# A CIN layer on one core: pairs 3 to 15 of its blocks as 32 by 64 matmul tiles, instead of 128 by 128 matmuls with a tiled remainder

## The chip, the cores and the metric

The kernel runs on one core of a Trainium2 chip. The metric is the device time of one execution in microseconds (us); the median of three runs before the change is 733.72 us. The engines are called as the profile calls them: PE (TensorE, matmuls), PEld (its weight loads), DVE (VectorE), ACT (ScalarE), POOL (GpSimd, which issues the gathers) and SP (SyncE, which issues plain DMAs).

## The reference

A batch of 1024 rows, 39 fields (F) and 64 elements (E) goes through three layers, all in float32:

```python
def _cin_layer(Xk, X0, W, b):
    O = W.shape[0]
    Hk, Fdim = (Xk.shape[1], X0.shape[1])
    Wr = W.reshape(O, Hk, Fdim)
    return jnp.einsum('bhe,bfe,ohf->boe', Xk, X0, Wr) + b[None, :, None]
X0 = sparse_embedding
Xk = X0
outs = []
for W, b in ((W0, b0), (W1, b1), (W2, b2)):
    Xk = _cin_layer(Xk, X0, W, b)
    outs.append(Xk.sum(axis=-1))
cin_output = jnp.concatenate(outs, axis=-1)
return cin_output @ fc_w.T + fc_b
```

Only the sums over e reach the output, so the kernel folds layers 2 and 3 and the final product into a second set of weights. What is left to compute for each column (b, e) is, for all unordered pairs of fields (a, b), the product x_a x_b times two sets of 64 weights (W0 and the folded set): 780 pairs and 39 linear terms.

## The kernel before, in words

**Blocks.** The batch is cut into 32 blocks of 32 rows, 2048 columns (32 x 64) each. Two consecutive blocks make a pair: blocks 0 and 1 are pair 1, blocks 30 and 31 are pair 16.

**Data.** `load(n)` copies block n from the input into one of three DRAM tables `xd`, laid out with fields as rows (a pair's two blocks one after the other). POOL then gathers rows of the table into SBUF by index lists (`gather_rows`, line 174): `roll(n)` fills five tiles of 128 partitions by 2048 columns (`rt[n % 2]`, two buffers), each a permutation of the fields with repeats, and `roll_small(n)` fills two tiles of 1024 columns, `ut` and `vt`, for a small remainder.

**Products.** A step (n, c) multiplies two of the five tiles elementwise on DVE (`product`, line 219, out tile `p`, four buffers). Six steps, c = 0 to 5, cover most field pairs in 128 partitions each. The rest of the field pairs fit in 32 partitions; for these the four partition groups of one product hold four column ranges of both blocks of a pair (line 221), so this seventh step comes once in a pair.

**Matmuls.** `multiply` (line 559) does four matmuls of 128 by 128 over 512 columns for a step, one for each of the four PSUM banks of the block (`po`). `join` does the remainder: 16 matmuls of 32 rows by 64 columns of weights (line 579) and, for the linear terms, eight more of the same shape (line 590). Eight such tiles fit side by side in the array. Each float32 matmul stands in the trace as two MATMUL and two LDWEIGHTS records, so a pair has 96 MATMUL records at line 559, 32 at line 579 and 16 at line 590.

**After the sums.** When a block's banks are complete, `finish` turns each of the four with one ACT instruction (line 607) and one DVE instruction (line 609) into a tile `g`, and a DVE reduction (line 620) sums over e, two for a block. ACT copies the fields into `g` (`fields`, line 602).

**Order.** The program is written out by hand, each engine works in order, and semaphores follow from data. The main loop walks the steps of one pair after another: multiply step `at` on PE, then make the product of step `at + AHEAD` (AHEAD is 4) on DVE. The gathers for a later block are emitted behind the last product that reads their buffer. SP's queue holds the loads; `load(n + 4)` waits there until every gather from the table that it overwrites has landed.

Of the kernel before, what the change touches and what calls it, by code (L numbers as in the profile page):

```python
# [39 lines left out]
NY = 3  # L87
YB = B // 4
# [59 lines left out]
def cin_kernel(ctx: ExitStack, tc: tile.TileContext, x, w0t, b0, w1, b1, w2, b2, fc_w, fc_b, out):  # L148
# [28 lines left out]

    def roll(n, tiles=range(NT)):
        for i in tiles:
            k = n % 2 * NT + i  # L180
            gather_rows(rt[n % 2][:, i], xd[n // 2 % NTAB][: FT if k < NT else 2 * FT], k)
# [19 lines left out]
    lists = const.tile([128, 2 * NT + 2], I32, name="lists")  # L201
    rt = [const.tile([128, NT, BLK], F32, name=f"r{k}") for k in range(2)]
# [10 lines left out]
    def product(n, c, cols=slice(0, BLK), p=None):  # L213
        if p is None:
            p = prods.tile([128, BLK], F32, name="p", tag="p")
        if c < NPAIR:
            i, k = PAIRS[c]
            r = rt[n % 2]
# [6 lines left out]
    with prep as prep:  # L225
# [8 lines left out]
        place = prep.tile([128, 1], I32, name="place")  # L234
# [63 lines left out]

        def step(x, at, by, out=None):
# [38 lines left out]
        nc.gpsimd.memset(bothv[0:H, :, F], 0.0)  # L338
        for h in (0, H):
# [40 lines left out]
        r, most, seat, far = (new() for _ in range(4))  # L380
# [92 lines left out]
        nc.vector.tensor_scalar(lists[:, 2 * NT :], both_of, 2.0, seat, ALU.mult, ALU.add)  # L473
        roll_small(0)
# [72 lines left out]
    work = ctx.enter_context(tc.tile_pool(name="work", bufs=2))  # L547
    sums = const.tile([H + F, B], F32, name="sums")
# [48 lines left out]

    def fields(n):
        g[n] = []
        for m in range(BLK // SUB):  # L600
            gt = work.tile([H + F, SUB], F32, name="g", tag="g")
            nc.scalar.copy(gt[H : H + F], rt[n % 2][0:F, 0, bass.ts(m, SUB)])  # L602
            g[n].append(gt)

    def finish_bank(n, m, z):
        one, other = slice(m % 2 * H, m % 2 * H + H), slice((m + 1) % 2 * H, (m + 1) % 2 * H + H)
        nc.scalar.activation(z[one], po[n][m][other], AF.Identity, bias=fc0s[other])  # L607
        at = bass.ts(m % 2, MM)
        return lambda: nc.vector.scalar_tensor_tensor(  # L609
            g[n][m // 2][0:H, at], po[n][m][one], b0s[one], z[one], ALU.add, ALU.mult  # L610
        )

    def finish(n):
        z = [work.tile([128, MM], F32, name="z", tag="z") for _ in range(BLK // SUB)]
        then = [finish_bank(n, m, z[m // 2]) for m in range(BLK // MM)]
        for m in range(BLK // MM):
            then[m]()
            if m % 2:
                b_at = n * BB + m // 2 * SB
                nc.vector.tensor_reduce(  # L620
                    sums[:, b_at : b_at + SB],
                    g[n][m // 2].rearrange("p (b e) -> p b e", e=E),
                    AX.X,
                    ALU.add,
                )

    def finish_quarter(n, m):
        z = work.tile([128, MM], F32, name="z", tag="z")
        finish_bank(n, m, z)()
# [23 lines left out]
    TAIL = 2  # L653
    steps = []
# [151 lines left out]
```

## Time and profile before

| | |
|---|---|
| runs | 732.83, 733.72, 734.34 us; median 733.72 |
| span of the profiled execution | 731.4 us, first to last instruction |
| its own time beside the span | not listed apart from the three runs, which lie 1.4 to 2.9 us above the span |
| PE busy | 724.7 us (99%) |
| DVE busy | 638.3 us (87%) |
| POOL busy | 397.6 us (54%) |
| ACT busy | 166.9 us (23%) |
| moved by DMA | 197.24 MB, mean 270 GB/s |

A row of the groups reads: line, engine, operation, names out<-in, shapes, count, then busy time and the mean of one in ns, then idle time before them. A row of the timeline reads: start, duration, engine, line, operation, count. Matmuls overlap, so the mean duration of one (some 600 ns) is longer than the distance from one start to the next, and it is the distances that add up to the time.

### The profile page before, as it was taken

Reading aid. Unit: us, or ns where it says so; the run is one execution under the profiler, and the core shown is the slowest. Engines: PE = TensorE matmul, PEld = TensorE weight load, DVE = VectorE, ACT = ScalarE, POOL = GpSimd, SP = SyncE. Lnnn points to the kernel's source line nnn. Section 1 sums busy time; section 2 is a strip of 40 time slices with the busy share of each in tenths; the row PEclk is TensorE's granted clock in tenths of the full one; section 3 lists DMA queues with packets and bytes.
Section 4 is the critical chain, followed back from the end, with each engine's and each line's share of the span. In section 5 each row is a group of like instructions: output and inputs, shape, how many; then the busy total and the mean of one; then the engine's idle time right before and its main releaser. Section 6 shows DMA issues by size and latency. Waiting matters only on the chain.

```text
span 731.4 us, 6351 instructions
## 1 busy us (share of the span) xinstructions
PE 724.7 (99%) x2375; PEld 316.1 (43%) x2375; DVE 638.3 (87%) x521; ACT 166.9 (23%) x240; POOL 397.6 (54%) x254
## 2 busy tenths in 40 slices
PE   8999999999999999999999999999999999999998
PEld 4444444444444444444444444444444444444443
DVE  6999798988889988889988889888898988889885
ACT  3332121222212222221222212222121221212222
POOL 6789886536555445754537555455654547545300
PEclk9999999999999999999999999999999999999999
DMA  8997899789575887757679675896767777565700
GB/s 268 376 337 280 315 342 356 290 307 338 232 273 231 281 336 286 270 225 285 269 288 330 223 289 219 304 348 236 268 256 274 301 287 266 224 252 236 288 0 0
DMA packets 65983, 197.24 MB, mean 270 GB/s; under 512 B 40110, under 2 KB 40179, under 8 KB 45984
## 3 DMA queue, kind: packets, MB, share of 16 engines
q0 software_dynamic: 28784, 185.56, 65.5%
q1 hardware_dynamic: 35468, 9.29, 5.5%
q10 hardware_dynamic: 1700, 1.99, 1.0%
q8 instruction: 18, 0.29, 0.1%
q14 instruction: 13, 0.11, 0.0%
HBM read 196.76 MB, written 10.60 MB: 284 GB/s over the span
## 4 chain that ended last, share of the span: by engine, by line
PE 99%; DVE 0%; DMA 0%; issue 0%; ACT 0%; DVEq 0%
PE po L559 91%; PE po L579 4%; PE po L590 2%; PE idle L279 0%; PE pv L406 0%; PE pt L487 0%; PE small L323 0%; PE pv L487 0%; PE pw L418 0%; DMA fcrow<-in_fc_w 0%; PE tr L543 0%; DVE g L609 0%; DVE pairs L526 0%; DVE sums L631 0%; ACT z L607 0%
## 5 line engine op out<-in xcount | busy, mean ns | idle before, releaser
L559 PE MATMUL po<-p,wa 128*128 128x512 f32 x1536 | 666.0, 594 | 0.0
L219 DVE TENSOR_TENSOR p<-r 128x2048 f32<-128x2048 f32 (+2 forms) x198 | 434.1, 2224 | 72.4 <-PE po L559 67.1
L559 PEld LDWEIGHTS po<-p,wa 128*128 128x128 f32 x1536 | 290.5, 190 | 371.7 <-issue 354.6
L174 POOL DMA_INDIRECT r<-xd,lists x156 | 302.3, 1938 | 267.1 <-issue 266.2
L607 ACT ACTIVATE z<-po,columns 64x512 f32<-64x512 f32 x128 | 87.3, 682 | 380.1 <-PE po L590 217.9
L609 DVE SCALAR_TENSOR_TENSOR g<-po,b0s,z 64x512 f32<-64x512 f32 x128 | 95.9, 749 | 9.3 <-ACT z L607 5.3
L602 ACT COPY g<-r 39x1024 f32<-39x1024 f32 x64 | 66.7, 1043 | 155.0 <-DVE sums L620 126.8
L620 DVE TENSOR_REDUCE sums<-g 103x16 f32<-103x1024 f32 x62 | 75.6, 1220 | 2.1
L174 POOL DMA_INDIRECT u<-xd,lists x16 | 38.9, 2432 | 7.5 <-issue 4.6
L174 POOL DMA_INDIRECT v<-xd,lists x16 | 38.5, 2403 | 4.9 <-issue 4.9
L579 PE MATMUL po<-p,wa 32*64 32x512 f32 x512 | 31.6, 600 | 0.0
L221 DVE TENSOR_TENSOR p<-u,v 128x1024 f32<-128x1024 f32 x16 | 19.5, 1218 | 0.0
L579 PEld LDWEIGHTS po<-p,wa 32*64 32x64 f32 x512 | 9.4, 131 | 20.2 <-issue 19.4
L590 PE MATMUL po<-u,wa 32*64 32x512 f32 x256 | 17.0, 587 | 0.0
L174 POOL DMA_INDIRECT r<-xh,lists x8 | 8.0, 996 | 4.8 <-DVE tmp L387 2.7
L590 PEld LDWEIGHTS po<-u,wa 32*64 32x64 f32 x256 | 5.7, 132 | 8.0 <-issue 8.0
L526 DVE TENSOR_TENSOR pairs<-both 128x2 f32<-128x2 f32 (+27 forms) x59 | 6.1, 171 | 0.2
L544 ACT COPY wa<-tr 128x128 f32<-128x128 f32 x8 | 2.1, 266 | 16.2 <-PE tr L543 16.2
L279 PE MATMUL idle<-const-float32-1.0 128*128 128x256 f32 (+1 forms) x8 | 4.0, 596 | 0.8 <-PEq L793 0.8
L543 PE MATMUL tr<-unit,pairs 128*128 128x128 f32 x8 | 2.4, 294 | 2.2 <-DVE pairs L526 2.2
L543 PEld LDWEIGHTS tr<-unit,pairs 128*128 128x128 f32 x8 | 1.2, 151 | 4.7 <-ACT pairs L524 2.7
L168 POOL DMA_DIRECT2D xd<-in_x x3 | 3.2, 1055 | 0.0
(97 smaller groups left out, 56.7 us busy)
## 6 DMA issues: line engine op xcount, KB each, us to landing
xd<-in_x SPq DMA_DIRECT2D x28, 312.0 KB
r<-xd,lists POOLq DMA_INDIRECT x156, 8.9
xd<-in_x POOLq DMA_DIRECT2D x3, 312.0 KB, 7.6
w2s<-in_w ACTq DMA_DIRECT2D x1, 624.0 KB
w1s<-in_w ACTq DMA_DIRECT2D x1, 624.0 KB
w0s<-in_w0t ACTq DMA_DIRECT2D x1, 380.2 KB
xh<-in_x ACTq DMA_DIRECT2D x2, 156.0 KB
xd<-xh SPq DMA_DIRECT2D x2, 156.0 KB
```

What stands on the lines that cost most here:

```text
L174: nc.gpsimd.indirect_dma_start(dst, None, table, bass.IndirectOffsetOnAxis(ap=lists[:, k : k + 1], axis=0))
L219: nc.vector.tensor_tensor(p[:, cols], r[:, i, cols], r[:, k, cols], ALU.mult)
L221: nc.vector.tensor_tensor(p[:, 0:SUB], ut[n // 2 % 2], vt[n // 2 % 2], ALU.mult)
L279: nc.tensor.matmul(idle[:, 0:cols], nc.const_aps.tensor(1.0, (128, 128), F32), nc.const_aps.tensor(1.0, (128, cols), F32), start=True, sto ...
L526: nc.vector.tensor_tensor(out, diagonal(a, b, sa, sb), diagonal(b, a, sb, sa), ALU.add)
L559: nc.tensor.matmul(po[n][m], wa[:, c, side : side + 2 * H], p[:, bass.ts(m, MM)], start=n % 2 == 0 and c == 0, stop=n % 2 == 1 and c == NP ...
L579: nc.tensor.matmul(dst[half * H : half * H + H], wa[rows, NPAIR, at : at + H], p[rows, bass.ts(side, MM)], start=t >= 2, stop=t < 2 and ha ...
L590: nc.tensor.matmul(dst[half : half + H], wa[rows, NPAIR + 1, H : 2 * H], ut[n // 2 % 2][rows, bass.ts(side, MM)], start=False, stop=t < 2,)
L602: nc.scalar.copy(gt[H : H + F], rt[n % 2][0:F, 0, bass.ts(m, SUB)])
L607: nc.scalar.activation(z[one], po[n][m][other], AF.Identity, bias=fc0s[other])
L609: return lambda: nc.vector.scalar_tensor_tensor(g[n][m // 2][0:H, at], po[n][m][one], b0s[one], z[one], ALU.add, ALU.mult)
L620: nc.vector.tensor_reduce(sums[:, b_at : b_at + SB], g[n][m // 2].rearrange("p (b e) -> p b e", e=E), AX.X, ALU.add,)
```

## The change

Pairs 1, 2 and 16 stay as they are. In pairs 3 to 15 (13 pairs) every matmul has the 32 by 64 form. A pair's 4096 columns are cut into four ranges of 1024, one for each group of 32 partitions. A gathered slot is a tile of 128 partitions by 1024 columns, in which group s holds 32 fields of range s; 14 such slots (`slot`, `gather_slots`) take the place of the 12 gathered tiles. Four slots with shifts 0 to 3 times one slot with shift 3, 7, 11, 15 or 19 give a product of 4 x 512 columns with one DVE instruction whose second operand is broadcast (`part_product`); a sixth group is made of the slots with the seven left fields, and one half-size step ("odd") is the rest. A pair has 13 steps as before: 12 products of 2048 columns and one of 1024.

Each unit of 512 columns of such a product is multiplied by eight matmuls, four partition groups by two halves (`part_multiply`), and the linear terms by eight more (`part_linear`). Four groups go to four banks; a pair has two sets of four, one for each half of the columns.

The weights are put in order once, during pair 2: `part_rows` copies and adds them into `pairs` with 21 DVE and 6 ACT instructions, `part_turns` transposes them with 7 PE transposes into `wc`, and 12 DMAs on SP copy them to the other three partition groups (`wn`). The index list of the slots, `narrow`, is worked out in the prologue by 14 POOL memsets and 16 small DVE instructions. Field rows of `g` come by four DMAs for a pair from the table (`part_fields`) instead of four ACT copies, and the reductions are spread over later steps, one to a step.

The order of PE in the middle of a pair before, from the end of the remainder's tiles (L579, L590) to the next full matmuls:

```order
L579 MATMUL po<-p,wa 64x512
L579 MATMUL po<-p,wa 64x512 [waits Activation_49]
L579 MATMUL po<-p,wa 64x512
L590 MATMUL po<-u_87,wa 64x512 [waits DMASW7_49]
L590 MATMUL po<-u_87,wa 64x512 x7
L559 MATMUL po<-p,wa 128x512 [waits DVE_49]
L559 MATMUL po<-p,wa 128x512 x3
L559 MATMUL po<-p,wa 128x512 [waits DVE_49]
```

The order of PE in the changed kernel in the middle of pair 3: the linear terms (L767), and behind them the next product's matmuls (L754), with weights from `wc` or `wn`:

```order
L767 MATMUL po<-r_87,wn 64x512 [waits DMASW2_49]
L767 MATMUL po<-r_87,wn 64x512
L767 MATMUL po<-r_87,wc 64x512 x2
L767 MATMUL po<-r_87,wn 64x512 x4
L754 MATMUL po<-p,wc 64x512 [waits DVE_49]
L754 MATMUL po<-p,wc 64x512
L754 MATMUL po<-p,wn 64x512 x8
L754 MATMUL po<-p,wc 64x512 x2
```

The form no longer alternates with a 128-row one, and an instruction covers a quarter of the rows and half of the weight columns.

PE at the border of pairs 2 and 3 before (the first two rows are the last step but one of pair 2, and the wait for ACT is that for free banks):

```order
L559 MATMUL po<-p,wa 128x512 [waits DVE_49]
L559 MATMUL po<-p,wa 128x512 x3
L559 MATMUL po<-p,wa 128x512 [waits DVE_49]
L559 MATMUL po<-p,wa 128x512 x3
L559 MATMUL po<-p,wa 128x512 [waits DVE_49,Activation_49]
L559 MATMUL po<-p,wa 128x512 [waits Activation_49] x3
```

PE at the same border in the changed kernel, from the last transposes (L679) on; L569 is the former L559, and a DMAHW wait is one for a DMA that SP issued:

```order
L679 MATMUL po<-unit,pairs 128x128 x2
L569 MATMUL po<-p,wa 128x512 x8
L569 MATMUL po<-p,wa 128x512 [waits DVE_49]
L569 MATMUL po<-p,wa 128x512 x3
L569 MATMUL po<-p,wa 128x512 [waits DVE_49]
L569 MATMUL po<-p,wa 128x512 x3
L754 MATMUL po<-p,wc 64x512 [waits DVE_49,Activation_49,Pool_49]
L754 MATMUL po<-p,wc 64x512
L754 MATMUL po<-p,wn 64x512 [waits DMAHW7_49,Activation_49]
L754 MATMUL po<-p,wn 64x512
L754 MATMUL po<-p,wn 64x512 [waits DMAHW0_49,PE_49]
```

Transposes stand four steps ahead of the border, and the first matmuls behind it wait for the copies of the weights.

SP's queue before, from the first load of pair 3's successor on (`xd_68`, `xd_69`, `xd_70` are the three tables; a DMASW wait is one for a gather):

```order
L168 DMA xd_68<-in_x 1248x1x64 [waits DMASW6_49,DMASW5_49,DMASW7_49,DMASW4_49,DMAHW3_49,DMASW3_49,DMAHW6_49,DMASW2_49,DMAHW7_49,DMASW1_49,DMASW0_49]
L168 DMA xd_68<-in_x 1248x1x64 [waits DMAHW4_49]
L168 DMA xd_69<-in_x 1248x1x64 [waits DMASW4_49,DMASW5_49,DMASW3_49,DMASW6_49,DMASW2_49,DMAHW1_49,DMASW1_49,DMASW0_49]
L168 DMA xd_69<-in_x 1248x1x64 [waits DMAHW2_49]
L168 DMA xd_70<-in_x 1248x1x64 [waits DMASW4_49,DMASW5_49,DMASW3_49,DMASW6_49,DMASW2_49,DMASW7_49,DMASW1_49,DMASW0_49]
```

SP's queue in the changed kernel at the same place (L134 is the former L168):

```order
L134 DMA xd_68<-in_x 1248x1x64 [waits DMASW6_49,DMASW5_49,DMASW7_49,DMASW4_49,DMAHW3_49,DMASW3_49,DMAHW6_49,DMASW2_49,DMAHW7_49,DMASW1_49,DMASW0_49]
L134 DMA xd_69<-in_x 1248x1x64 [waits DMASW5_49,DMASW4_49,DMASW6_49,DMASW3_49,DMAHW1_49,DMASW2_49,DMAHW4_49,DMASW1_49,DMASW0_49]
L134 DMA xd_69<-in_x 1248x1x64 [waits DMAHW2_49]
L134 DMA xd_68<-in_x 1248x1x64
L689 DMA wn<-wc 32x896 [waits DVE_49,Activation_49,Pool_49]
L689 DMA wn<-wc 32x896 [waits DMAHW0_49]
L689 DMA wn<-wc 32x896 x2
L689 DMA wn<-wc 32x896 [waits DMAHW3_49]
L689 DMA wn<-wc 32x896 [waits DMAHW4_49]
L689 DMA wn<-wc 32x896 [waits DMAHW5_49]
L689 DMA wn<-wc 32x896 [waits DMAHW6_49]
```

The second load into `xd_68` (block 7) moved behind the two into `xd_69` (blocks 8 and 9), and the twelve copies of the weights stand behind all of them. SP and ACT hand out eight DMAHW numbers in turn, so that a DMA waits for the eighth before it. The first copy has number 7 (PE waits for it above), so the load of block 7 has number 6, and the eighth copy waits until that load has landed.

The diff's core (the shapes of the slots and the weights' 27 runs in `part_rows` are left out):

```diff
+TILES = 4
+ROWS = 128 // TILES
+NPART = NBLK // 2
+WHOLE = (0, 1, NPART - 1)
+SHIFT = (0, 1, 2, 3, 7, 11, 15, 19)
+NK, NG5 = 4, 5
...
+    def part_turns(k):
+        open_part(k, 0)
+        for q in range(NTURN):
+            at = q % 4 * 128
+            nc.tensor.transpose(po[2 * k][q // 4][:, at : at + 128], pairs[:, q], unit)
...
+        for u in range(TILES):
+            for s in range(TILES):
+                if s != u:
+                    nc.sync.dma_start(
+                        wn[ROWS * s : ROWS * s + ROWS, u], wc[ROWS * u : ROWS * u + ROWS]
+                    )
...
+    def gather_slots(k, *which):
+        table = xd[k % NTAB].rearrange("f (t c) -> (f t) c", c=SUB)
+        for j in which:
+            nc.gpsimd.indirect_dma_start(
+                slot(k, j),
+                None,
+                table,
+                bass.IndirectOffsetOnAxis(ap=narrow[:, j : j + 1], axis=0),
+            )
+
+    def part_product(k, group, side):
+        p = prods.tile([128, BLK], F32, name="p", tag="p")
...
+        nc.vector.tensor_tensor(
+            p.rearrange("p (k c) -> p k c", k=NK),
+            slots(k, many, NK, side),
+            slot(k, one)[:, bass.ts(side, MM)].unsqueeze(1).to_broadcast([128, NK, MM]),
+            ALU.mult,
+        )
+        return p, [(NK * group + j, side) for j in range(NK)]
...
+    def weights(c, s):
+        q, u = c // TILES, c % TILES
+        rows = slice(ROWS * s, ROWS * s + ROWS)
+        return wc[rows, q] if s == u else wn[rows, u, q]
+
+    def part_multiply(k, units, p, last):
+        for u, (c, side) in enumerate(units):
+            open_part(k, side)
...
+            for s in range(TILES):
+                rows = slice(ROWS * s, ROWS * s + ROWS)
+                for half in range(2):
+                    kind = (s + side + half) % 2 * H
+                    nc.tensor.matmul(
+                        po[2 * k + side][s][half * H : half * H + H],
+                        weights(c, s)[:, kind : kind + H],
+                        p[rows, bass.ts(u, MM)],
...
+    PART = (
+        *((0, 0), (1, 0), (0, 1), (1, 1), (2, 0), (2, 1), (3, 0), (3, 1), ("odd", 0)),
+        *((4, 0), (5, 0), (4, 1), (5, 1)),
+    )
     steps = []
-    for n in range(0, NBLK, 2):
-        steps += [(n, c) for c in range(NPAIR + 1)] + [(n + 1, c) for c in range(NPAIR)]
+    for k in range(NPART):
+        steps += whole_steps(k) if k in WHOLE else [(k, *t) for t in PART]
...
+        if (n, c) == (2, 0):
+            rows_due.extend(part_rows())
+        if (n, c) == (3, 1):
+            part_turns(first_part)
+
+    def part_step(k, group, side):
...
+        part_multiply(k, units_of.pop(step), p.pop(step), tail)
+        if (group, side) == (0, 1):
+            part_linear(k)
...
+        if tail:
+            part_finish(k, side)
+            sums_due.extend((k, side, b) for b in range(2))
...
+        middle = (2, 1) if len(step) == 3 else (NPAIR,)
+        k = step[0] if len(step) == 3 else step[0] // 2
+        if step[1:] == middle and 1 <= k and k + 3 < NPART:
+            load(2 * k + 6)
+            load(2 * k + 7)
```

More of the change, by code (lines that the diff above doesn't have):

```diff
@@ L338, in cin_kernel @@
         nc.gpsimd.memset(bothv[0:H, :, F], 0.0)
+        slot_shifts()
         for h in (0, H):
@@ L379, in cin_kernel @@
             )
-        r, most, seat, far = (new() for _ in range(4))
+        r, most, far = (new() for _ in range(3))
         both_of = prep.tile([128, 2], F32, name="both_of")
```

315 lines of the change are left out of this document (282 added, 33 removed).

## The prediction

> **What bounds the kernel now.** I read the page's busy line and chain first: is there one engine whose work is the time?
>
> ```profile
> PE 724.7 (99%) x2375; PEld 316.1 (43%) x2375; DVE 638.3 (87%) x521; ACT 166.9 (23%) x240; POOL 397.6 (54%) x254
> PE 99%; DVE 0%; DMA 0%; issue 0%; ACT 0%; DVEq 0%
> PE po L559 91%; PE po L579 4%; PE po L590 2%; PE idle L279 0%; PE pv L406 0%; PE pt L487 0%; PE small L323 0%; PE pv L487 0%; PE pw L418 0%; DMA fcrow<-in_fc_w 0%; PE tr L543 0%; DVE g L609 0%; DVE pairs L526 0%; DVE sums L631 0%; ACT z L607 0%
> ```
>
> PE is the chain from end to end: whatever makes PE quicker is gained in full, whatever makes it wait is paid in full. So the next view is PE's timeline, around one remainder and between two full matmuls far apart (starts first, durations second; the last row is the next pair's remainder).
>
> ```profile
> 348.81 0.59 PE L559 MATMUL po<-p,wa 128*128 128x512 f32 x1
> 349.34 1.97 PE L579 MATMUL po<-p,wa 32*64 32x512 f32 x32
> 351.53 0.63 PE L590 MATMUL po<-u,wa 32*64 32x512 f32 x8
> 352.10 4.13 PE L559 MATMUL po<-p,wa 128*128 128x512 f32 x9
> ...
> 359.50 1.02 PE L559 MATMUL po<-p,wa 128*128 128x512 f32 x2
> 384.82 0.59 PE L559 MATMUL po<-p,wa 128*128 128x512 f32 x1
> ...
> 393.49 1.97 PE L579 MATMUL po<-p,wa 32*64 32x512 f32 x32
> ```
>
> 384.82 - 359.50 = 25.32 us is 59 starts of 0.429 us. I call one such record, or a group of eight small ones side by side, a pass. The weight loads show that the small groups have the same beat:
>
> ```profile
> 349.82 0.18 PEld L579 LDWEIGHTS po<-p,wa 32*64 32x64 f32 x8 [0.25 <-issue]
> 350.25 0.18 PEld L579 LDWEIGHTS po<-p,wa 32*64 32x64 f32 x8 [0.25 <-issue]
> ```
>
> 0.43 us for eight. A pair has 96 + 48/8 = 102 passes: 43.76 us. From remainder to remainder it takes 393.49 - 349.34 = 44.15. The other 0.39 us is the change of form: 0.53 from the last full start to the first small one (0.10 too much), 0.57 from the last small group to the next full one (0.14 too much), the rest on the passes just behind.
>
> **The change: matmuls.** A changed pair has 50 units and one set for the linear terms, each eight tiles, each tile two records: 102 passes again. So the array's work is the same, and what goes is the change of form. Before there are 16 remainders; after, three (pairs 1, 2, 16) and one entry and one exit for all of pairs 3 to 15, so 4. 12 x 0.39 = 4.7 us gained, all of it on PE.
>
> Issue: a pass takes 16 PE instructions instead of two, 26.8 ns for each. The 96 instructions of one remainder take 352.10 - 349.34 = 2.76 us, 28.75 ns each, but that is the array's beat, and a queue could have held some. A burst behind a wait is nearer to the bare rate:
>
> ```profile
> 4.84 0.29 PEld L406 LDWEIGHTS pv<-w2s,fc 128*64 128x64 f32 x3 [0.27 <-DVE wide L362]
> 4.87 0.80 PE L406 MATMUL pv<-w2s,fc 128*64 128x320 f32 x2
> ```
>
> Both rows are of a window that ends at 4.90: five instructions have started within 0.06 us of 4.84, 12 to 15 ns each. I take the issue as hidden, at 0; the two ends are 0 and 16 x 28.75 = 0.46 us a pass, 0.031 x 13 x 102 = 41 us. [...]
>
> **Weights.** Seven transposes are added in pair 2. One in the prologue:
>
> ```profile
> 36.48 1.02 PE L559 MATMUL po<-p,wa 128*128 128x512 f32 x2
> 37.34 0.27 PE L543 MATMUL tr<-unit,pairs 128*128 128x128 f32 x1
> 37.45 1.02 PE L559 MATMUL po<-p,wa 128*128 128x512 f32 x2
> ```
>
> 0.11 us from its start to the next: 7 x 0.11 = 0.8 us, on PE. Their 21 DVE adds and 6 ACT copies are spread over pair 2 and bounded by DVE's spare time in a pair, below; I cost them at 0.
>
> **The entry of pair 3.** PE's first small tiles of pair 3 need the twelve copies `wn`, and these are last in SP's queue. PE in pair 2 (the first row is behind its remainder, the second its last record, with pair 3's first 0.43 us later), SP, POOL, and the page's row of POOL's loads (at its end the us from issue to landing):
>
> ```profile
> 87.15 7.13 PE L559 MATMUL po<-p,wa 128*128 128x512 f32 x16
> 107.42 1.02 PE L559 MATMUL po<-p,wa 128*128 128x512 f32 x2
> ...
> 89.11 0.78 SPq L168 DMA_DIRECT2D xd<-in_x  x1
> 89.94 9.61 SPq L168 DMA_DIRECT2D xd<-in_x  x1
> ...
> 82.00 1.04 POOL L168 DMA_DIRECT2D xd<-in_x  x1
> 92.39 0.94 POOL L174 DMA_INDIRECT r<-xd,lists  x1 [0.31 <-issue]
> 94.87 10.41 POOL L174 DMA_INDIRECT v<-xd,lists  x1 [0.30 <-issue]
> xd<-in_x POOLq DMA_DIRECT2D x3, 312.0 KB, 7.6
> ```
>
> Pair 3 begins at 107.85 before, 108.65 with the transposes. SP issues the loads of blocks 8 and 9 at 89.11 and 89.94 (they wait for pair 2's gathers, which the change leaves), and the second blocks SP for 9.61 us. New behind them: the load of block 7, and only then the twelve copies. How fast do loads come through beside gathers? The queues' shares (packets, MB, share of 16 engines; q0 is POOL's, q1 is SP's), in the windows 92 to 102, 93 to 106, 125.5 to 143.5 and 162.5 to 166.5 us:
>
> ```profile
> q0 software_dynamic: 547, 4.01, 94.8%
> q1 hardware_dynamic: 680, 0.17, 7.6%
> ...
> q0 software_dynamic: 643, 4.09, 74.8%
> q1 hardware_dynamic: 2522, 0.64, 21.7%
> ...
> q0 software_dynamic: 907, 5.46, 73.8%
> q1 hardware_dynamic: 2522, 0.64, 15.7%
> ...
> q1 hardware_dynamic: 2522, 0.64, 70.3%
> ```
>
> Two loads are 2522 packets. Alone they need 70.3% of 4 us, 2.8 us; beside gathers 13 to 18 us. Three are 3783 packets: 4.2 us alone, 20 to 27 us by the two contended windows, so from 93 to 113 or 120. The engines share out packets, not bytes (680 of SP's to 547 of POOL's), and POOL's take nearly all the time. [...]
>
> What limits this: pair 3's gathers are 14 x 128 x 4 KB = 7.3 MB, at 0.40 MB/us 18 us. All wait for block 5's load now, since a slot takes rows of both blocks: 82.00 + 7.6 = 89.6, so they run from some 91.5 to 110. Pair 4's gathers wait for block 7's load, so the pause that frees SP's packets comes then: 91.5 + 18.3 + 4.2 = 114 for the end of the load. I take 113, between the two ways. The eighth copy is issued only once that load has landed (its DMAHW number). What a small DMA of SP needs:
>
> ```profile
> 728.38 0.76 SPq L753 DMA_DIRECT2D out_y<-y  x1
> ```
>
> The output is issued at 728.38, and the span ends at 731.4: at most 3.0 us. 113 + 1 + 3 = 117 for the eighth copy, which PE wants at 108.65 + 4 x 0.43 = 110.4. The wait is 6.5 us, most of it at the first copy already. Its ends: 0, if the copies land by 108.65 (POOL slow, so that loads slip through), and 12, if the load ends at 119.
>
> Behind a wait PE's clock is lower. After 2.18 us of idling in the prologue (second row: PE's busy us behind the length, and near the end the granted clock):
>
> ```profile
> 16.43 0.30 PE L543 MATMUL tr<-unit,pairs 128*128 128x128 f32 x1 [2.18 <-DVE pairs L526]
> 16.50:20.00 3.50, 3.50 (x7) 1.54 (x8) 3.50 (x19) 0.96 (x6) 2.89 (x3) 0.55 1.02 389
> ```
>
> 3.5 us at 0.55 lose 1.6 us. I add 1.5 here, with 0 and 1.6 as ends. While PE waits, DVE can make only the four products it has buffers for, and POOL goes on; nothing is late next.
>
> **Steady pairs.** One pair (PE, PEld, DVE, ACT, POOL busy, clock, DMA share, GB/s), the small gathers, which have the new shape, the instruction queue, and two DVE groups of the prologue:
>
> ```profile
> 172.70:216.86 44.16, 44.16 (x145) 19.11 (x145) 38.94 (x25) 9.63 (x12) 23.39 (x12) 1.00 0.75 276
> L174 POOL DMA_INDIRECT u<-xd,lists x16 | 38.9, 2432 | 7.5 <-issue 4.6 <-DVE p L219 2.9
> q8 instruction: 18, 0.29, 0.1%
> L496 DVE STREAM_TRANSPOSE flat<-pt 128x320 f32<-128x320 f32 x2 | 1.0, 518 | 2.1 <-PE pt L487 2.1
> L526 DVE TENSOR_TENSOR pairs<-both 128x2 f32<-128x2 f32 (+27 forms) x59 | 6.1, 171 | 0.2
> ```
>
> DVE has 25 instructions for a pair as before, 38.94 us, beside a pair now 43.76 long: 4.8 us spare, and four products ahead. POOL issues 14 gathers instead of 12, at most 14 x 2.43 = 34 us. Gathered bytes fall from 11.5 to 7.3 MB, four field copies of 160 KB come back. ACT loses four copies. All hidden: 0; were DVE to run into PE, its cover is those 4.8 us. Instructions arrive in 16 KB pieces (0.29 MB in 18); PE's go from 288 to 1632 for a pair, and even six times the pieces are 1.7 MB beside 190, with a quarter of the DMA time free: 0. The prologue's list is 16 small DVE operations, 16 x 0.17 = 2.7 us by the last row, where DVE waits 2.1 us for PE by the row above it: 0 to 0.6, I take 0, since PE itself is waited for there; its memsets are POOL's, ahead of gathers that wait for the input.
>
> **Sum.** Span 731.4 - 4.7 + 0.8 + 6.5 + 1.5 = 735.5, 4.1 us more. The median of the runs, 733.72, lies 2.3 above the span; with the same 4.1, 737.8 us.
>
> **Rivals.**
> - The copies come in time: the wait is under 2.3 us. Mechanism: POOL's gathers in the new shape are slow (2.43 + 0.30 us, 14 in 38 us, 0.19 MB/us), so DMA is half free and 3783 packets take some 9 us, 93 to 102; copies land at 107. For it: that mean. Against: the row at 92.39 with 0.94 us, and that gathers before fill the engines to 94.8%. Then 733.7 - 4.7 + 0.8 + (0 to 2.3) = 729.8 to 732.2; likeliest 730. The turning point: load 7 ended by about 107.
> - A wait of 2.3 to 3.6 us cancels the gain with the clock's loss: 732.3 to 735.1, no change.
> - PE is bound by issue. For it: eight times the instructions. Against: the burst. 733.7 - 3.9 + 41 = 771 us, whatever the entry does.
> - Little changes because the change of form costs as much inside the small form (weights from two tiles, four banks): then only the entry is left, and it is slower still; within the forecast's upper part.
>
> **Chances.** A wait of 3.6 to 12 us: 0.55, forecast 737.8, its own range 735 to 743.5. The copies in time: 0.25. In between: 0.11. Issue: 0.07. Anything else that leaves the time: 0.02. What a measurement tells from no change is 0.2%, 1.5 us. Faster 0.25, same 0.13, slower 0.55 + 0.07 = 0.62. The range takes the first three cases: 730.0 to 743.5.
>
> **What would show it.** In the trace after: starts of small groups at 0.43 us throughout (step one) and no 0.53 or 0.57 in pairs 3 to 15; 43.8 us a pair. Before pair 3 an idle PE with a DMA of `wn` as the releaser, 6 us long, then some 3.5 us at half clock. POOL's gathers of pair 4 start after block 7's load, near 114. The prediction is wrong if PE idles less than 2 us there, if groups stand 0.46 us apart or more, or if PE waits for DVE or gathers in later pairs.

## The result: 761.26 us, and the profile after

The changed kernel takes 761.26 us (median of 6 runs, 758.0 to 765.34), the kernel before beside it 733.95 (6 runs, 732.83 to 736.21): a ratio of 1.037, interval 1.034 to 1.040. The prediction was 737.8, with 743.5 as its upper end. Ratios below leave out runs over 1.5% above the fastest of their kernel, and medians do not, so that the two can differ.

The page of the changed kernel, its busy line and its chain by engine:

```profile
PE 732.3 (96%) x11118; PEld 336.8 (44%) x11118; DVE 633.5 (83%) x558; ACT 114.5 (15%) x196; POOL 508.8 (67%) x294
issue 30%; POOL 30%; PE 16%; DMA 10%; DVE 2%; SPq 1%; ACT 0%; POOLq 0%; DVEq 0%; ACTq 0%
```

Before, the chain was 99% PE. Now POOL has 30% of it, and PE 16%. The waits of PE and of DVE (us in total, times, longest) say what PE lacks:

```profile
PE po L754 <- DVE p L722: 15.6, 10, 2.3
PE po L754 <- DMA wn<-wc: 2.6, 2, 1.4
PE po L754 <- DVE p L726: 1.8, 8, 0.2
...
DVE p L722 <- DMA v<-xd,narrow: 79.7, 10, 8.4
```

Ten times, once in each of pairs 5 to 14, PE waits for the odd product (L722), and this product has waited some 8 us for the slot `v`, which POOL gathers. The wait that was predicted, for the copies `wn`, is there too.

**The pairs.** The linear terms (L767) come once in a pair, so the distance of their first records is a pair's length. Windows from one to the next, the pairs that start at 169.63, 213.40 and 353.31 (us, then busy PE, PEld, DVE, ACT, POOL, granted clock, DMA share, GB/s):

```profile
169.63:213.40 43.77, 43.77 (x828) 29.22 (x820) 37.90 (x26) 5.46 (x8) 31.07 (x14) 1.00 0.57 188
213.40:259.33 45.93, 45.10 (x833) 22.91 (x824) 37.62 (x26) 5.46 (x8) 31.74 (x15) 1.00 0.59 190
353.31:398.75 45.44, 44.29 (x825) 18.39 (x817) 37.33 (x26) 5.47 (x8) 31.44 (x15) 1.00 0.60 192
```

The first of these is as predicted, 43.77, and so is the pair ahead of it, 43.78. The next ten, pairs 5 to 14, take 464.0 us (213.40 to 677.41) instead of 437.8. That is 26.2 us, nearly the whole loss. The third row shows that neither DVE (37.33 busy) nor POOL (31.44) is full.

**What holds `v`.** POOL, DVE and PE in the third of these pairs (start, duration, count, idle time before):

```profile
348.30 14.72 POOL L712 DMA_INDIRECT r<-xd,narrow  x1 [0.30 <-issue]
363.32 0.94 POOL L712 DMA_INDIRECT r<-xd,narrow  x1 [0.30 <-issue]
364.56 0.94 POOL L712 DMA_INDIRECT v<-xd,narrow  x1 [0.30 <-issue]
```

```profile
347.74 4.47 DVE L726 TENSOR_TENSOR p<-r 128x2048 f32<-128x2048 f32 x2
352.14 1.20 DVE L800 TENSOR_REDUCE sums<-pairs 103x16 f32<-103x1024 f32 x1
353.27 2.27 DVE L726 TENSOR_TENSOR p<-r 128x2048 f32<-128x2048 f32 x1
...
359.93 2.27 DVE L726 TENSOR_TENSOR p<-r,u 128x2048 f32<-128x2048 f32 x1
362.12 1.20 DVE L800 TENSOR_REDUCE sums<-g 103x16 f32<-103x1024 f32 x1
371.18 1.23 DVE L722 TENSOR_TENSOR p<-u,v 128x1024 f32<-128x1024 f32 x1 [7.86 <-DMA v<-xd,narrow]
```

```profile
372.46 0.64 PE L754 MATMUL po<-p,wc 32*64 32x512 f32 x2 [0.92 <-DVE p L722]
```

A gather that nothing holds takes POOL 0.94 us. One in each pair takes 14.72. It lies under a run of DVE in which product, product, then four reductions and three products by turns follow each other without a pause, and it ends at 363.02, 0.82 us behind the end of the last product (359.93 + 2.27 = 362.20). The gather of `v` is the second behind it. The transfers thin out meanwhile and then come all at once (same columns as above):

```profile
353.31:366.00 12.69, 12.69 (x248) 5.48 (x240) 10.02 (x7) 0.00 (x0) 11.78 (x4) 1.00 0.29 90
366.00:372.50 6.50, 5.58 (x109) 2.05 (x94) 1.32 (x2) 0.00 (x0) 2.63 (x3) 1.00 0.99 331
```

The DMA share is 0.29, then 0.99; `v` lands at 371.2, the product follows, and PE has idled by then. The group of these gathers shows none of it:

```profile
L712 POOL DMA_INDIRECT r<-xd,narrow x130 | 319.7, 2459 | 155.2 <-DVE p L726 111.9
```

The mean is 2459 ns, and the prediction's from the kernel before was 2432.

In the kernel before, the longest gather of a steady pair is this one, beside these products:

```profile
362.51 4.47 POOL L174 DMA_INDIRECT r<-xd,lists  x1 [7.77 <-issue]
363.89 4.53 DVE L219 TENSOR_TENSOR p<-r 128x2048 f32<-128x2048 f32 x2
```

It also ends 0.8 us behind a product (363.89 + 2.29 = 366.18; gather's end 366.98). There a reduction followed its finishing instructions; the change took the reductions from there and put one into each of the later steps, between products. That is in the diff (`sums_due`), and the prediction gave it no term.

**The entry of pair 3.** SP's rows, then the queues' shares of the DMA engines (packets, MB, share) in 92 to 100 and in 100 to 115 us:

```profile
91.04 3.23 SPq L134 DMA_DIRECT2D xd<-in_x  x3
100.21 7.79 SPq L689 DMA_DIRECT2D wn<-wc  x12
```

```profile
q1 hardware_dynamic: 3783, 0.96, 52.8%
q0 software_dynamic: 311, 1.16, 42.3%
...
q0 software_dynamic: 735, 2.68, 63.5%
q1 hardware_dynamic: 592, 1.41, 36.9%
```

All 3783 packets of the three loads are through by 100, not by 113. The twelve copies are issued one behind the other, 0.65 us each, from 100.21 to 108.0, and share the engines with pair 3's gathers. What the first of them waits for is on ACT, which copies the transposed weights from PSUM to `wc`:

```profile
98.10 1.04 ACT L811 COPY g<-r 39x1024 f32<-39x1024 f32 x1 [1.78 <-DVE sums L834]
99.17 0.97 ACT L682 COPY wc<-po 128x512 f32<-128x512 f32 x2
```

The transposes are done at 94.55, but ahead of the copy to `wc` ACT has a field copy that waits for a DVE reduction; `wc` is ready at 100.14, and SP issues 0.07 us later. PE from pair 2's remainder on, and windows from pair 3's start on:

```profile
83.69 1.97 PE L589 MATMUL po<-p,wa 32*64 32x512 f32 x32
93.43 1.12 PE L679 MATMUL po<-unit,pairs 128*128 128x128 f32 x7
108.21 0.64 PE L754 MATMUL po<-p,wc 32*64 32x512 f32 x2
111.39 1.18 PE L754 MATMUL po<-p,wn 32*64 32x512 f32 x6 [1.21 <-DMA wn<-wc]
115.19 2.36 PE L754 MATMUL po<-p,wn 32*64 32x512 f32 x6 [1.39 <-DMA wn<-wc]
125.85 0.59 PE L767 MATMUL po<-r,wn 32*64 32x512 f32 x2
108.20:121.54 13.34, 10.75 (x105) 4.70 (x112) 12.83 (x9) 0.69 (x2) 11.51 (x7) 0.74 1.03 272
115.19:121.54 6.35, 6.35 (x52) 3.33 (x60) 6.11 (x5) 0.00 (x0) 5.72 (x3) 0.51 1.03 300
```

From the start to the linear terms are 24 passes, 10.30 us. They took 17.64: the entry loses 7.34 us. Of these 2.6 are idle time that the waits show; 6.35 us at a granted clock of 0.51 lose some 3.1, an estimate; the other 1.6 lie ahead of 115.19, where the matmuls start in pieces behind the copies. The 7.34 us are called the entry's loss below. It doesn't count what is lost ahead of the first product of pair 3; for that, the way from pair 2's remainder (L589) to the linear terms is given too, here 125.85 - 83.69 = 42.2 us.

### The profile page after: what moved, and what is told of

Its sections match the earlier page's. It is cut to its first block, busy times and chain, and to the rows that moved or that the text cites. A ratio compares the mean times of both kernels' runs of the same rounds, so it can differ in the third digit from the quotient of the medians.

```text
span 761.0 us, 24003 instructions
## 1 busy us (share of the span) xinstructions
PE 732.3 (96%) x11118; PEld 336.8 (44%) x11118; DVE 633.5 (83%) x558; ACT 114.5 (15%) x196; POOL 508.8 (67%) x294
## 3 DMA queue, kind: packets, MB, share of 16 engines
q8 instruction: 87, 1.43, 0.8%
## 4 chain that ended last, share of the span: by engine, by line
issue 30%; POOL 30%; PE 16%; DMA 10%; DVE 2%; SPq 1%; ACT 0%; POOLq 0%; DVEq 0%; ACTq 0%
POOL r L712 26%; PE po L754 10%; DMA r<-xd,narrow 7%; PE po L569 5%; POOL u L712 2%; POOL v L712 2%; DMA wn<-wc 1%; DMA r<-xd,lists 1%; SPq L689 1%; DMA v<-xd,narrow 1%; DVE g L818 0%; DVE sums L834 0%; DVE p L191 0%; DVE p L726 0%; PE po L589 0%
## 5 line engine op out<-in xcount | busy, mean ns | idle before, releaser
L754 PE MATMUL po<-p,wn 32*64 32x512 f32 x7800 | 575.5, 593 | 2.6 <-DMA wn<-wc 2.6
L754 PE MATMUL po<-p,wc 32*64 32x512 f32 x2600 | 556.6, 593 | 17.4 <-DVE p L722 15.6
L712 POOL DMA_INDIRECT r<-xd,narrow x130 | 319.7, 2459 | 155.2 <-DVE p L726 111.9
L754 PEld LDWEIGHTS po<-p,wn 32*64 32x64 f32 x7800 | 247.3, 133 | 219.1 <-issue 186.0
L754 PEld LDWEIGHTS po<-p,wc 32*64 32x64 f32 x2600 | 171.6, 133 | 108.1 <-issue 64.5
L726 DVE TENSOR_TENSOR p<-r 128x2048 f32<-128x2048 f32 x78 | 176.0, 2282 | 6.5 <-PE po L754 2.4
L569 PE MATMUL po<-p,wa 128*128 128x512 f32 x288 | 126.8, 597 | 0.0
L726 DVE TENSOR_TENSOR p<-r,u 128x2048 f32<-128x2048 f32 x52 | 118.5, 2280 | 3.9 <-PE po L754 3.9
L722 DVE TENSOR_TENSOR p<-u,v 128x1024 f32<-128x1024 f32 x13 | 15.9, 1224 | 86.4 <-DMA v<-xd,narrow 79.7
L191 DVE TENSOR_TENSOR p<-r 128x2048 f32<-128x2048 f32 (+2 forms) x42 | 81.7, 1978 | 6.7 <-DMA r<-xd,lists 5.7
L569 PEld LDWEIGHTS po<-p,wa 128*128 128x128 f32 x288 | 54.1, 191 | 68.5 <-issue 63.8
L140 POOL DMA_INDIRECT r<-xd,lists x26 | 65.4, 2517 | 12.3 <-issue 6.7
L726 DVE TENSOR_TENSOR p<-r,v 128x2048 f32<-128x2048 f32 x26 | 59.4, 2284 | 4.5 <-PE po L754 4.5
L140 POOL DMA_INDIRECT u<-xd,lists x3 | 17.0, 5683 | 2.3 <-DVE p L191 1.7
```

The lines of the kernel that those rows point to most:

```text
L140: nc.gpsimd.indirect_dma_start(dst, None, table, bass.IndirectOffsetOnAxis(ap=lists[:, k : k + 1], axis=0))
L191: nc.vector.tensor_tensor(p[:, cols], r[:, i, cols], r[:, k, cols], ALU.mult)
L569: nc.tensor.matmul(po[n][m], wa[:, c, side : side + 2 * H], p[:, bass.ts(m, MM)], start=n % 2 == 0 and c == 0, stop=n % 2 == 1 and c == NP ...
L712: nc.gpsimd.indirect_dma_start(slot(k, j), None, table, bass.IndirectOffsetOnAxis(ap=narrow[:, j : j + 1], axis=0),)
L722: nc.vector.tensor_tensor(p[:, 0:SUB], slot(k, LEFT), slot(k, RIGHT + NK), ALU.mult)
L726: nc.vector.tensor_tensor(p.rearrange("p (k c) -> p k c", k=NK), slots(k, many, NK, side), slot(k, one)[:, bass.ts(side, MM)].unsqueeze(1) ...
```

## The experiments

The theory: the lone reductions between products keep POOL's gather out, and what stands behind it comes late. The rivals: the new slots or products by themselves; DVE is simply too busy; the order of the gathers; the entry, whose delay is carried on. All runs are timed beside the kernel before; diffs are against the changed kernel.

**Reductions back beside the finishing instructions (e1).** `part_sum` right behind each two instructions of `part_finish`:

```diff
+            if s % 2:
+                part_sum(k, side, s // 2)
...
-            sums_due.extend((k, side, b) for b in range(2))
```

> The changed kernel, with the four reductions of a pair back beside the finishing instructions, two behind each pair of them, instead of one to a step between products. Theory (DVE's run without a gap, two products and then product and reduction by turns, keeps one POOL gather waiting 14.7 us in every pair, and the two slots of the odd product are behind it): the run is broken by the finishing instructions and by waits for PE, no gather takes over 8 us, the odd product stops waiting for v, pairs take 43.8 us, and the 26 us of pairs 5 to 15 go: 735 to 738 us. Rival (fourteen gathers a pair are simply too many for POOL, at 2.3 us each beside DVE): 758 to 762 us, as it is. Second rival (reductions in a burst make products late, and PE waits for DVE instead): 740 to 758 us, with PE waiting for products other than the odd one.

Measured: 750.18 us, ratio 1.022 (1.015 to 1.028). No wait for the odd product is left. But a long hold is, elsewhere (POOL and DVE):

```profile
347.57 12.61 POOL L712 DMA_INDIRECT v<-xd,narrow  x1 [0.31 <-issue]
348.29 6.69 DVE L726 TENSOR_TENSOR p<-r 128x2048 f32<-128x2048 f32 x3
354.89 4.49 DVE L726 TENSOR_TENSOR p<-r,u 128x2048 f32<-128x2048 f32 x2
```

Five products in a row hold as well (359.38 + 0.8 = 360.18). So lone reductions are not needed for a hold: here a run of products does it. Each pair takes 44.63 us, 0.86 too much. In the pair shown it is lost between 345.5 and 347.7, where PE begins the next pair's third product and DVE's finishing instructions, now with reductions between them, end at 347.11; that PE waits there for the banks that they free is argued from these times and not shown. The expected 735 to 738 us did not come. The time lies in the range of the second rival, but its sign is missing: PE has no wait for a product in pairs 3 to 15.

**The odd product's slots ahead of the right ones (e2).** In the list of the last step's gathers:

```diff
-                (5, 1): (LEFT, *range(RIGHT, RIGHT + NK + 1)),
+                (5, 1): (LEFT, RIGHT + NK, *range(RIGHT, RIGHT + NK)),
```

> The changed kernel, with one gather moved: the second slot of the odd product is gathered ahead of the four slots of the sixth group instead of behind them. Nothing else moves, and the count is the same. Theory: the gather held 14 to 15 us is still there in every pair, but the odd product's slots are ahead of it, so DVE doesn't wait 8 us for v, and what is behind the hold is wanted later: 735 to 740 us. Rival (too many gathers): the same POOL time is only met at another product, 756 to 762 us.

Measured: 735.63 to 758.95 in nine runs, median 751.25; the ratio of 1.0066 (1.0037 to 1.0095) is that of the three shortest, up to 742.16. In the profiled execution, a long one of 748.06, nine pairs take 43.77 or 43.78 though the hold is there,

```profile
344.16 14.73 POOL L712 DMA_INDIRECT r<-xd,narrow  x1 [0.30 <-issue]
```

since what it delays is now used later. e12 below, with the same order, shows it in a whole execution: a hold of 14.72 us in each pair, and all pairs at 43.77 or 43.78. So it is not the hold that costs, but what is behind it in POOL's queue. The version has no margin: later in the execution of 748.06 us the hold grows to 19.2 us, and pairs to 47.9.

**Copies ahead of the loads (e3).** Loads 7, 8 and 9 are issued behind the twelve copies:

```diff
-        if c == 0 and n in (2, 3):
+        if c == 0 and n == 2:
...
+            for m in (7, 8, 9):
+                load(m)
...
-        if step[1:] == middle and 1 <= k and k + 3 < NPART:
+        if step[1:] == middle and 2 <= k and k + 3 < NPART:
```

> The changed kernel, with the loads of blocks 7, 8 and 9 put behind the twelve copies of the weights in SP's queue instead of ahead of them. Theory of the entry (PE loses 7.3 us there, waiting for copies that stand behind three loads, and by the lower clock after it): the loss falls to under 1.5 us. If the rest is as it was: 754 to 756 us. Rival: from pair 5 on POOL's gathers set the pace, so that an earlier entry is only waited for later: 758 to 761 us, although the entry's loss is gone.

Measured: 762.74 us, 1.038 (1.034 to 1.042). Neither of the two expected ranges came. The copies are issued at 103.70, in e2 at 103.62 (both executions reach pair 2's remainder 2.5 to 3 us later than the changed kernel's); ACT's copy to `wc` ends at 103.63: it was not the loads that they waited for. The entry's loss falls to 1.72, but PE waits 3.08 us for the first product of pair 3, and from pair 2's remainder to the linear terms are 40.2 us, only 2.0 fewer than in the changed kernel. The steady pairs lose no less than there (20.3 us of waits for the odd product, 15.6 there). The entry is a matter of its own.

**The kernel before, its reductions spread one to a step (e5).**

```diff
-            if m % 2:
-                ... nc.vector.tensor_reduce(...)
+        sums_due.extend((n, m) for m in range(2))
...
+        if sums_due and at - 1 not in over:
+            due = sums_due.pop(0)
+            sum_up(*due)
```

> The kernel before, with its reductions taken from beside the finishing instructions and put one to a step behind products, as the change does. Theory (a run of DVE without a gap holds a gather): gathers longer than 8 us appear in every pair, where the longest in steady pairs was 4.5; the kernel before has 20 us of POOL's time to spare in a pair, so the time is 732 to 738 us. Rival (the long gather belongs to the new slots, their count or their rows): no gather in steady pairs over 5 us, 732 to 736 us.

Measured: 736.6 us, 1.0048 (1.0033 to 1.0063). The longest gather from 110 us on is 5.22 us, and 2.28 from 130 on, not over 8: a miss. In the kernel before it is 4.48 there, so the holds became shorter. DVE and POOL, in a stretch of 11.4 us without a pause (356.44 to 367.81: product, product, then reduction and product twice by turns):

```profile
360.85 1.21 DVE L624 TENSOR_REDUCE sums<-g 103x16 f32<-103x1024 f32 x1
362.04 2.34 DVE L219 TENSOR_TENSOR p<-r 128x2048 f32<-128x2048 f32 x1
362.05 0.94 POOL L174 DMA_INDIRECT r<-xd,lists  x1 [0.30 <-issue]
```

Five gathers pass in this stretch, none above 2.27 us. So lone reductions and a DVE without pauses do not make a hold of 14 us by themselves. The rival's sign (no gather over 5 us in steady pairs) is met, but its cause, the new slots, is not: in the changed kernel a gather of the old form (L140, at 673.22) is held for 19.18 us beside the new products. A rival that no run tries is the form of the product itself, whose second operand is now broadcast (L726).

**Shorter reductions (e7).** Each reduces 16 of 64 elements:

```diff
-            g[k, side, b].rearrange("p (h b e) -> p h b e", h=2, e=E),
+            g[k, side, b].rearrange("p (h b e) -> p h b e", h=2, e=E)[:, :, :, 0 : E // 4],
```

> The changed kernel, with the four reductions of pairs 3 to 15 cut to the first 16 of 64 elements of each row (three quarters of the reduction are left out); gathers, products and order are the same. DVE has 3.6 us less to do in a pair. Theory (what holds POOL is DVE's run without a gap): the run ends sooner, the held gather takes under 12 us instead of 14.7, the waits for the odd product fall by more than half: 735 to 748 us. Rival (the number of gathers alone): 757 to 762 us.

Measured: 739.11 us, 1.0079 (1.0049 to 1.0109); every pair takes 43.77 or 43.78. The hold is 9.81 us and ends when DVE, quicker now, runs out of work and waits 1.03 us for PE. Less work on DVE cures it, then; this alone would also fit a DVE that is too busy.

**Reductions by twos (e13).** The same reductions, the same DVE work, two behind each other instead of one:

```diff
-            due = sums_due.pop(0)
+            for _ in range(2 if len(sums_due[0]) == 3 else 1):
+                due = sums_due.pop(0)
```

> The changed kernel with the reductions two to a step, so that two stand together between products, instead of one and one. It tells what keeps POOL out between two products. If POOL gets in whenever DVE has no product under way, a 2.4 us stretch of reductions lets the held gather go after the first or second pair of products: under 8 us instead of 14.7, and the time falls to 735 to 755 us. If POOL is kept out for as long as a next product already stands ready behind the running instructions, the hold stays at 14 to 17 us and the time at 755 to 764 us.

Measured: 737.67 us, 1.0036 (1.0008 to 1.0065). POOL, DVE and one steady pair:

```profile
340.69 4.74 POOL L712 DMA_INDIRECT r<-xd,narrow  x1 [0.31 <-issue]
345.74 4.15 POOL L712 DMA_INDIRECT v<-xd,narrow  x1 [0.30 <-issue]
350.19 7.49 POOL L712 DMA_INDIRECT r<-xd,narrow  x1 [0.30 <-DVE sums L800]
```

```profile
340.14 4.48 DVE L726 TENSOR_TENSOR p<-r 128x2048 f32<-128x2048 f32 x2
344.54 1.21 DVE L800 TENSOR_REDUCE sums<-pairs 103x16 f32<-103x1024 f32 x1
345.67 1.20 DVE L800 TENSOR_REDUCE sums<-both 103x16 f32<-103x1024 f32 x1
346.79 2.27 DVE L726 TENSOR_TENSOR p<-r 128x2048 f32<-128x2048 f32 x1
```

```profile
608.31:652.08 43.77, 43.77 (x830) 19.58 (x822) 38.50 (x26) 5.46 (x8) 24.95 (x12) 1.00 0.54 175
```

The first gather ends at 345.43, 0.81 behind the two products; no wait for the odd product is left; all pairs take 43.77 or 43.78, with DVE as busy as ever (38.50). This separates the theory from "DVE too busy": only the places of the reductions differ, and DVE has no more pauses in this stretch than before. The numbers are now those of the prediction: span 736.5 (735.5 predicted), entry's loss 8.0 (8.0 predicted, of other parts).

**Slots by SP instead of POOL (e6).** Four of the 14 slots come by 16 plain DMAs:

```diff
+                nc.sync.dma_start(
+                    slot(k, j)[ROWS * s : ROWS * s + ROWS],
+                    xd[k % NTAB][first : first + ROWS, s % 2 * SUB : s % 2 * SUB + SUB],
+                )
```

> The changed kernel, with four of a pair's fourteen slots (shifts 0 to 3, whose rows are consecutive) fetched by sixteen plain DMAs of SP instead of four gathers of POOL, from pair 5 on. Bytes and work are the same. Theory (POOL is short of time: it is held while DVE runs without a gap, and must fill most slots between their last use in one pair and their first in the next): with ten gathers POOL catches up, the odd product waits for nothing, pairs take 43.8 us, the entry's loss of 7 to 8 us stays: 735 to 739 us. Rival (it is the bytes and the landing of small rows, not POOL's time): 755 to 762 us.

Measured: 738.78 us, 1.0058 (1.0026 to 1.009). Pairs take 43.77 to 44.38, and the longest steady gather 7.2 us: the hold is shorter, in one pair because its gather starts 8 us later in DVE's run (344.03, the run 335.96), and fewer gathers stand behind it.

**The entry: copies on two queues (e10, e11, e12, e14).** Half of the twelve are issued by ACT:

```diff
-                    nc.sync.dma_start(
+                    (nc.scalar if s % 2 else nc.sync).dma_start(
```

e10 is e6 with it; e11 has two slots by SP and e2's order beside it; e12 e2's order; e14 the reductions by twos.

> As the run with four slots by SP, with the twelve copies of the weights issued half by SP and half by ACT, and nothing else. At the entry SP took 0.63 us to issue each copy. If the issue is what delays them, the entry's loss falls from 7 to 8 us to 3 to 4, and the time with it, 731 to 735 us. If the copies share the DMA engines with the gathers of pair 3, packet by packet, and that is what delays them, the loss stays at 6 to 8 us and the time at 735 to 739.

> The changed kernel with three edits: two of fourteen slots (shifts 0 and 1) by eight DMAs of SP instead of two gathers, the odd product's slots gathered ahead of the sixth group's, and the copies of the weights half on SP and half on ACT. With four slots by SP, PE had lost 0.2 to 1.1 us at a few places where it waited for nothing that the profile shows, each 2.3 to 3.0 us behind a packet of the instruction queue; half as many DMAs should leave fewer of these. Theory: 43.8 us a pair, no entry loss, under 2 us at such places: 729.5 to 732.5 us, faster than before by up to 0.5%. Rival (twelve gathers beside DVE are still too many in some executions): 733 to 745 us.

> The changed kernel with the odd product's slots gathered first and the copies of the weights on two queues; all fourteen gathers stay on POOL. Theory: pairs of 43.8 us while POOL keeps up, entry loss under 1 us; but with a gather held 14.7 us in each pair POOL has next to nothing to spare, and in some executions it falls behind in late pairs: between 729 us (all pairs in time) and 750 us, with a wide spread from run to run. Rival (the spread came from the entry): 729 to 733 us in all runs.

> The changed kernel with the reductions two to a step, and the copies of the weights half on SP and half on ACT; all gathers stay on POOL. Theory: pairs of 43.8 us (as with the reductions by twos alone), and an entry loss between the 0.05 and 4.6 us that two queues gave in other runs, instead of 7 to 8: 730 to 735 us. Rival (the entry's loss is the sharing of the DMA engines with pair 3's gathers, and two queues only helped by chance): 736 to 740 us.

| | us | ratio | entry's loss in the profiled execution |
|---|---|---|---|
| e10 | 737.84 | 1.0038 (1.0003 to 1.0072) | 0.05 |
| e11 | 736.46 | 1.0014 (0.9982 to 1.0046) | 5.7 |
| e12 | 735.61 | 0.9985 (0.9955 to 1.0015) | 4.6 |
| e14 | 733.4 | 0.9994 (0.9966 to 1.0021) | 1.7, and 3.10 of waiting for the first product |

From pair 2's remainder to the linear terms are 34.7 us in e10, 41.3 in e11, 39.2 in e12 and 40.7 in e14. So two queues can be enough (e10) and need not be: they alone do not settle the entry, and the single runs of each spread over 8 us and more. Of e12's ten runs four took 741.23, 752.7, 761.76 and 1978.05 us, and its ratio is that of the other six; the wide spread was expected, the entry's loss of under 1 us was not met. e11's median is in its rival's range, e14's in the range expected; e10's loss and median together fit neither of its two cases. In e10 PE also stops four times with "issue" as the releaser, 1.8 us in all, and each stop ends 2.5 to 3.0 us behind the start of an instruction transfer. That they belong together is seen from the times alone and not shown; of the kernels here only e6, e8 and e10 have such stops, those with four slots by SP.

**And pair 3's gathers out of the way (e8, e15).** e8 is e10 with e3's order of loads, e2's order of gathers, and the load of block 5 given to SP instead of POOL; e15 is e14 with the loads of e3 and

```diff
-                load(n + 4, nc.gpsimd)
+                load(n + 4, nc.sync if n else nc.gpsimd)
```

> As the run with four slots by SP, and with the entry of pair 3 relieved: the copies of the weights half on SP and half on ACT, ahead of the loads of blocks 7 to 9, the load of block 5 early on SP instead of on POOL, and the odd product's two slots gathered first. Theory: pairs of 43.8 us from pair 3 on and an entry loss under 2 us, so 733.7 - 4.6 + 0.9 + 1: 729 to 732 us, faster than before by 0.3 to 0.6%. Rival (some other wait takes the place of these): 733 us or more.

> As the run before it, and the loads of blocks 7 to 9 behind the copies, and the load of block 5 early on SP instead of on POOL, so that pair 3's gathers don't wait for it and are mostly done when the copies run. Theory: entry loss under 1 us, pairs of 43.8 us: 729 to 732 us, faster than before by 0.2 to 0.6%. Rival (an earlier load only crowds the gathers of pairs 1 and 2): entry gained, but as much lost ahead of it, 732 to 736 us.

Measured: e8 733.99 us, 0.9995 (0.9967 to 1.0024), its rival's range; the entry loses 0.05, and its pairs take 43.8 to 44.7, with stops of PE for "issue" as in e10. e15 takes **729.23 us** (727.88 to 731.32), ratio 0.9946 (0.9926 to 0.9966): it beats both kernels, the one before by 0.5%. (e14 and e15 ran on another chip than the rest; the kernel before took 733.37 there.) Its busy line, and PE from pair 3's start to the linear terms:

```profile
PE 718.5 (99%) x11118; PEld 309.4 (43%) x11118; DVE 636.5 (88%) x558; ACT 114.3 (16%) x196; POOL 477.5 (66%) x293
107.77 0.65 PE L754 MATMUL po<-p,wc 32*64 32x512 f32 x2
118.12 0.59 PE L767 MATMUL po<-r,wn 32*64 32x512 f32 x2
```

118.12 - 107.77 = 10.35, for 10.30 without any wait, and from pair 2's remainder on it is 34.7 us. All pairs take 43.77 or 43.78. Only two terms of the prediction are left, 731.4 - 4.6 + 0.9 = 727.7; the span is 726.7.

## Why the prediction was wrong, step by step

- **The matmuls: right.** A pair without waits takes 43.77 or 43.78 us, predicted 43.76, against 44.15 before: twelve times that is 4.6, predicted 4.7. e15 is faster by it.
- **Issue hidden: right.** Groups start 0.429 us apart where nothing is waited for, 16 PE instructions in each, so 26.8 ns an instruction are sustained over 13 pairs. The 28.75 ns at the upper end of the prediction, 0.46 us a pass, are not seen.
- **The transposes: right.** From 93.43 to the next full matmul at 94.38: 0.95 us, predicted 0.8.
- **The entry: its size right by luck, its cause wrong.** 8.0 predicted, 7.3 measured. Predicted were a wait of 6.5 us and 1.5 us at a lower clock; measured were some 4.2 and 3.1 (2.6 + 1.6 and 3.1 above). The step that failed is the time for three loads beside gathers, 20 us: it took the gathers of pair 3 to fill the engines from 92 on, and so the load's end at 113. Their first was issued at 92.75, they moved 1.16 MB up to 100 us, where 0.40 MB/us would have been 3.2, and the loads were through by 100, as in the rival in which the copies come in time (93 to 102). What the copies waited for is a step that the prediction did not have: ACT's copy to `wc`, done at 100.14. And they had a cost that no step had: 0.65 us of SP's queue each, 7.8 in all, and the gathers beside them. With the loads moved alone (e3) the copies come no earlier; with two queues and block 5's load moved forward as well (e8, e15) the loss is gone. In e10 it is gone with two queues alone (its slots by SP begin with pair 5), so which part of these edits does it stays open. No run moves ACT's copy ahead of the field copies.
- **The steady pairs: wrong.** "All hidden: 0" measured 26.2 us, and this one step explains the miss: 735.5 + 26.2 - 0.7 (entry) + 0.15 (transposes) = 761.15, measured 761.0. The prediction asked whether POOL and DVE have time enough, and they have. It did not ask when one gather comes back, what is behind it, and how soon the next user of a slot with one buffer wants it. It priced a gather at the mean of 2.43 us, which after the change is nearly the same and hides fourteen gathers of which one takes 14.72. And it costed 25 DVE instructions "as before" without looking at where the reductions had gone.

The runs agree that DVE keeps POOL's gathers back, and not for one instruction but for up to nine (14.72 us): where DVE's work or its order was edited, the hold became 12.61 us (e1) and 9.81 (e7), and in e13 the three gathers shown take 4.74, 4.15 and 7.49. Whether plain DMAs of SP escape it was not shown; in e6, where SP fetches four slots from pair 5 on, PE waits for a product once in pairs 3 to 15, 2.3 us.

What stays open: what exactly lets a gather in. In the kernel before it is let in behind a product while the next product is already running (rows above, 366.98); in e1 it stays out through five; in e5 it passes lone reductions that keep it out in the changed kernel. The runs show which orders of DVE's instructions end the hold, not why, and whether the form of the new product matters was not tried. PE's waits (15.6 + 1.8 us) do not make up the whole 26.2. In seven of the ten pairs PE is busy for 44.29 or 44.30 us, 0.5 more than 43.77; in part because a wait counts as idle only from the end of the last matmul, 0.59 us behind its start, where the next group is due after 0.43. In the pairs from 305.61 and 445.44 it is busy for 45.73 us, at a mean granted clock of 0.96:

```profile
326.26:329.67 3.41, 3.41 (x40) 1.30 (x32) 3.41 (x2) 0.00 (x0) 0.00 (x0) 0.50 0.96 240
```

Behind the waits of 1.97 and 2.00 us in these two pairs the clock was 0.50 for 3.4 us, which loses some 1.4 us more in each, a cost of late products that the prediction had at the entry alone. Only the 0.8 us more of the pair from 213.40 (45.10 busy at a clock of 1.00) are left without an explanation.

## What to carry to other kernels

An engine's spare time in a stage says nothing about one instruction in it: for every gather that POOL issues, look at its longest duration and not at the mean, and at what stands behind it for a buffer that is used at once. When a change moves small DVE instructions between large ones, ask what it does to the runs in which DVE never pauses; two reductions side by side were worth 3% here against the same two apart. Small DMAs that open a stage cost their queue some 0.65 us each here, so twelve in one queue have to start 8 us ahead; six on SP and six on ACT took 5.0 and 4.9 us in e15, not half. And look at what the first of them waits for, on every engine that hands its data on.

## What the runs showed of the hardware

- A gather of 0.94 us was held for 14.72 us by nine DVE instructions in a row, for 12.61 by five products, for 4.74 where two reductions followed two products, and took at most 2.27 beside products of the old form with lone reductions between them (e5). Each of these four ends 0.8 us behind the end of a product.
- Behind two waits of 1.2 and 1.4 us at the entry the granted clock was 0.51 over 6.35 us. Behind waits of 1.97 and 2.00 us in steady pairs it was 0.50 for 3.4 us; in the pairs with waits of 2.17 and 2.28 us (at 419.15 and 559.26) it stayed at 1.00. The length of a wait alone did not decide it.
- Instructions come in pieces, 87 of them (1.43 MB) instead of 18, and in the changed kernel PE did not stop for them once: none of its waits has "issue" as the releaser.
